# The next image's attention as side work inside a selective scan, with the depthwise taps on TensorE

## The chip, the cores and the metric

The kernel runs on one core of one Trainium2 chip. A time is the device time of one execution in microseconds. Three executions of the kernel before took 20170.54, 20181.5 and 20199.03 us; the time before is their median, 20181.5 us. One further execution was taken by the profiler, and all rows of the profile come from it.

## The reference

The input is a batch of 8 images of 384 channels and 64 x 64 positions, in fp32. Two layers follow each other, each added to its input.

Layer 0 is a channel attention on the group-normalised image (32 groups of 12 channels):

```python
q = dwconv3x3(conv1x1(gn(x), wq), dwq)      # likewise k and v; 9 taps per channel
q, k = l2norm(q), l2norm(k)                 # along the 4096 positions
attn = softmax(q @ k.T * temperature)       # 8 heads of 48 x 48 channels
x = x + conv1x1(attn @ v, wproj)
```

Layer 1 is a selective scan over the positions in four directions k (rows, columns, rows backward, columns backward):

```python
u = cross_scan(gn(x))                       # 4 directions x 384 channels x 4096 positions
dt, B, C = split(x_proj @ u)                # 12, 16, 16 rows
dt = softplus(dt_proj @ dt + dt_bias)
h = h * exp(dt * A) + (dt * u) * B          # for each of 16 states, position after position
y = sum over states of h * C, plus Ds * u
x = x + gelu(layernorm(cross_merge(y)))
```

## The kernel before

Channels lie on 128 partitions in three blocks (NJ = 3). The images are worked off one after the other: `channel_attention(b)`, then `selective_scan(b)`. The last step of an image (layer norm over channels, GELU, addition, store: `token_norm` and `finish_part`) is worked off inside the attention of the next image, through `emit`, and for the last image by `finish` at the end.

**Attention.** The whole image x lies in SBUF (three tiles of 4096 positions). `conv` multiplies x by the weights on TensorE (PE), into one of three PSUM banks `pc` (line 226), and ScalarE (ACT) copies with the bias into `pre` (line 231). The nine taps of the depthwise convolution are mainly multiply-adds on VectorE (DVE), one instruction for each tap and stretch of rows (line 266); for parts of the image the three taps of the middle column are matmuls with diagonal matrices on PE (line 249). `to_tokens` transposes (line 290), the gram matrix of q and k is summed on PE (line 327), and `project_out` multiplies, adds to x and takes statistics (lines 375 to 382). x1, the result, stays in SBUF and is stored for the finish.

**Scan.** An image has 32 steps: 4 directions times 8 chunks of 512 positions. A step has 12 units: 3 channel blocks times 4 groups of 4 states. A step's projection is `px` (line 474: for each of four stretches of 128 positions, matmuls with the x_proj weights of 44 columns; x is read in place, for odd k with a stride of 64), a copy to `xd`, `pd` (line 527: three matmuls of 128x512 with dt_proj) and softplus (line 535) to `dt`. GpSimd (POOL) computes `w` = dt * u (line 544). B comes back through DRAM as a copy on every partition (`fetch`, line 518), C as a spread tile `cp` (line 512). One unit u is:

- `drive`: POOL multiplies w by four rows of B, 128x2048 (`db`, line 573)
- `decay`: ACT computes four exponentials (`da`, line 561), in three PSUM banks
- `scan`: DVE runs four scans of 512 positions (`h`, line 585)
- `turn`: PE transposes h of the unit before, four sets of four transposes (`pt`, line 606), in two PSUM banks
- `keep`: ACT copies each set to SBUF (`hc`, line 614; one set of 48 in a step by DVE, line 616)
- `add_up`: PE multiplies each set by `cp` with 32 columns and sums in `py` (line 627; line 633 adds the term Ds * u with the matrix `skip`)

`take` adds py to what lies in DRAM (`ys`, `yd`, lines 655, 669, 653). `unit(u)` writes the order out by hand, and `tc.keep_in_program_order` holds every engine to it. Unit r = 9 of a step is the burst, in which the next step's pd and softplus run, with two table loads on ACT. A matmul in fp32 is two records in the profile, a transpose one.

Of the kernel before, what the change touches and what calls it, by code (L numbers as in the profile page):

```python
# [9 lines left out]
F32 = mybir.dt.float32  # L10
# [5 lines left out]
P = 128  # L16
C = 384
# [12 lines left out]
XR = R + 2 * N  # L30
# [49 lines left out]
def tile_channel_attention_then_selective_scan(ctx: ExitStack, tc: tile.TileContext, a: dict):  # L80
# [5 lines left out]
    big = ctx.enter_context(tc.tile_pool(name="big", bufs=1))  # L86
# [22 lines left out]
    for j in range(NJ):  # L109
        nc.vector.tensor_scalar_mul(skip[:, j, :], ident, d_sum[:, j : j + 1])  # L110

# [53 lines left out]
    def channel_attention(b, x, stats, before):  # L165
# [5 lines left out]
        with ExitStack() as st:  # L171
# [175 lines left out]
            emit = None  # L347
            if before is not None:
                scale, shift = token_norm(b, wp, work, before[2])

                def emit(i):
                    t = work.tile([P, L], F32, tag="acc", name=f"fin{b}_{i}")
                    room = [t[:, n * FT * NJ : (n + 1) * FT * NJ] for n in range(3)]
                    finish_part(*before, i, scale, shift, room, ps_t, "pt")

# [13 lines left out]
            x1_d = dram.tile([NJ, P, L], F32, tag="x1d", bufs=2, name=f"x1d{b}")  # L369
# [16 lines left out]
            todo, left, edges = [], list(range(L // FT)) if emit else [], {}  # L386
            for y0, y1 in zip(parts, parts[1:]):
                for m in range(NJ):
# [11 lines left out]
                    for _ in range(min(len(left), 2)):  # L400
                        emit(left.pop(0))
# [5 lines left out]
    def selective_scan(b, x1, stats1):  # L407

        y_d = dram.tile([L, C], F32, tag="yd", bufs=2, name=f"yd{b}")
        with ExitStack() as st:  # L410
            wp = st.enter_context(tc.tile_pool(name=f"sw{b}", bufs=1))
            work = st.enter_context(tc.tile_pool(name=f"s{b}", bufs=2))
            ps_y = st.enter_context(tc.tile_pool(name=f"sy{b}", bufs=2, space=PSUM))
            ps_a = st.enter_context(tc.tile_pool(name=f"sa{b}", bufs=3, space=PSUM))
            ps_t = st.enter_context(tc.tile_pool(name=f"st{b}", bufs=2, space=PSUM))
            ps_m = st.enter_context(tc.tile_pool(name=f"sm{b}", bufs=1, space=PSUM))
            pin = tc.keep_in_program_order

            wx = wp.tile([P, NJ, K, XR], F32, name=f"wx{b}")
            nc.sync.dma_start(wx, a["x_proj"])  # L420

            wdt = wp.tile([P, K, C], F32, name=f"wdt{b}")
            nc.gpsimd.memset(wdt, 0.0)  # L423
            nc.sync.dma_start(wdt[:R], a["dt_proj"])
            xd_bufs = [wp.tile([P, CH], F32, name=f"xd{b}_{i}") for i in range(2)]
            for t in xd_bufs:
                nc.gpsimd.memset(t, 0.0)

            with tc.tile_pool(name=f"sn{b}", bufs=1) as np_:
                mean, rstd = norm_factors(np_, ps_t, stats1, f"1_{b}", "t")  # L430
                shift = np_.tile([P, NJ], F32, name=f"shift{b}")
                nc.vector.tensor_mul(shift, mean, rstd)
                nc.vector.tensor_scalar_mul(shift, shift, -1.0)
                for c in range(NCH):
                    for j in range(NJ):
                        s = x1[j][:, bass.ts(c, CH)]
                        if c < 2:
                            nc.scalar.activation(  # L438
                                s, s, AF.Identity, bias=shift[:, j : j + 1],
                                scale=rstd[:, j : j + 1],  # L440
                            )
                        else:
                            nc.vector.tensor_scalar(
                                s, s, mean[:, j : j + 1], rstd[:, j : j + 1],
                                ALU.subtract, ALU.mult,
                            )

            def view(t, k, c):

                if k % 2 == 0:  # L450
                    return t[:, bass.ts(c, CH)].rearrange("p (x y) -> p x y", y=W)
                return t.rearrange("p (h w) -> p w h", w=W)[:, bass.ts(c, CH // H), :]

            def split(t):
                return t.rearrange("p (x y) -> p x y", y=W)

            steps = []
            for k in range(K):
                order = range(NCH) if k < 2 else range(NCH - 1, -1, -1)
                steps += [(k, c, i == 0, i == NCH - 1) for i, c in enumerate(order)]  # L460
            S = len(steps)
            UN = NJ * NG
            U = S * UN
            pxs, xds, bc_ds, cxs, pcts, cps, dts, ws, bts = {}, {}, {}, {}, {}, {}, {}, {}, {}

            def project(s, i):

                j, f = divmod(i, PX)
                k, c = steps[s][:2]
                if i == 0:  # L470
                    pxs[s] = ps_m.tile([P, CH], F32, tag="m", name=f"px{b}_{s}")
                n = CH // W // PX
                part = slice(f * n, (f + 1) * n)
                pin(nc.tensor.matmul(  # L474
                    split(pxs[s][:XR, :])[:, part, :], lhsT=wx[:, j, k, :],
                    rhs=view(x1[j], k, c)[:, part, :], start=i == 0, stop=i == PX * NJ - 1,
                ))

            def lay_out(s):

                xd = xd_bufs[s % 2]
                pin(nc.scalar.copy(xd[:XR, :], pxs.pop(s)[:XR, :]))  # L482
                bc_d = dram.tile([2 * N, CH], F32, tag="bcd", bufs=3, name=f"bcd{b}_{s}")
                nc.sync.dma_start(bc_d, xd[R:XR, :])
                cx = work.tile([NG * NQ, NV, HP], F32, tag="cx", bufs=1, name=f"cx{b}_{s}")
                for g in range(NG):
                    nc.sync.dma_start(
                        cx[g * NQ : (g + 1) * NQ],
                        bc_d[N + NV * g : N + NV * (g + 1), :].rearrange("v (q l) -> q v l", l=HP),
                    )  # L490
                xds[s], bc_ds[s], cxs[s] = xd, bc_d, cx

            def mingle_c(s):

                cy = work.tile([NG * NQ, HP, NV], F32, tag="cy", bufs=1, name=f"cy{b}_{s}")
# [3 lines left out]
            def turn_c(s):  # L499

                pcts[s] = ps_m.tile([P, CH], F32, tag="m", name=f"pct{b}_{s}")
# [5 lines left out]
            def spread_c(s, g):  # L507

                t = work.tile([P, NQ, HP], F32, tag="cp", bufs=5, name=f"cp{b}_{s}_{g}")
# [5 lines left out]
            def fetch(s, g):  # L515

                bts[s, g] = work.tile([P, NV, CH], F32, tag="B", bufs=NG, name=f"B{b}_{s}_{g}")
# [4 lines left out]
            def step_matmul(s, j):  # L522

                k = steps[s][0]
                pool, tag = (ps_m, "m") if j == 0 else (ps_t, "t")
                pd = pool.tile([P, CH], F32, tag=tag, name=f"pd{b}_{s}_{j}")
                pin(nc.tensor.matmul(  # L527
                    pd, lhsT=wdt[:, k, bass.ts(j, P)], rhs=xds[s], start=True, stop=True
                ))
                return pd  # L530

            def step_size(s, j, pd):
                k = steps[s][0]
                dts[s, j] = work.tile([P, CH], F32, tag="dt", bufs=4, name=f"dt{b}_{s}_{j}")
# [384 lines left out]
```

## Time and profile before

| what | us |
|---|---|
| median of three runs (20170.54 to 20199.03) | 20181.5 |
| the profiled execution's own time | 20193.86 |
| its span, first to last instruction | 20192.0 |
| first scan instruction (line 585) of image 0 and of image 1 | 488.2 and 2998.1 |
| scan of one image (488 to 2515) | 2027 |
| attention of one image with the finish of the image before (2515 to 2998) | 483 |
| after the last scan (20085 to 20192) | 107 |

In a row of a group, "busy" is the time in which at least one of its instructions ran, and "mean ns" the mean length of one. PE is the matmuls, PEld the loads of the weights that go before them. A row "A <- B" of the waits says that an instruction of A stood idle until one of B was done. A row of the timeline has the start, the length, the engine, the line, the operation with its tiles and how many instructions are merged in it; PE's rows can overlap, since a matmul's tail runs beside the next one.

### The profile page before, as it was taken

What the parts mean: (1) busy time and instruction counts of PE and PEld (TensorE: products, weight loads), DVE (VectorE), ACT (ScalarE), POOL (GpSimd) and SP (SyncE); (2) the same over time, 40 slices, a digit from 0 to 9 for tenths busy, and PEclk for the clock granted to TensorE, in tenths of its full rate; (3) what the DMA queues carried; (4) which work ended last, traced back from release to release, by engine and by line L of the source; (5) the groups of instructions that cost most, each with busy time, mean ns of one, the idle gap of its engine ahead of it and who ended that gap; (6) DMA issues with size and microseconds to landing.
All of it is one profiled execution on the core that took longest, in us unless ns stands there. A gap on an engine that the chain in (4) does not pass through costs nothing. (4 is left out here: it accounts for less than half of the span.)

```text
span 20192.0 us, 414595 instructions
## 1 busy us (share of the span) xinstructions
PE 17186.0 (85%) x167376; PEld 10318.0 (51%) x167376; DVE 18980.5 (94%) x17326; ACT 16767.4 (83%) x29099; POOL 15497.8 (77%) x6798
## 2 busy tenths in 40 slices
PE   7888888888888888888888888888888888888887
PEld 4555545555455544555545554455554555445554
DVE  7999989999899998999989999899998999989998
ACT  3999849998499985999859998599985999859998
POOL 0999909998099981999819998199971999729997
PEclk9999989999899999999999999899999999999998
DMA  1222322223222232222322223222232222322223
GB/s 43 84 95 94 99 78 84 94 95 101 75 84 95 94 105 78 84 94 96 103 74 85 95 94 102 74 85 95 94 102 74 85 95 95 102 75 85 94 94 121
DMA packets 1194159, 1814.03 MB, mean 90 GB/s; under 512 B 153552, under 2 KB 1018064, under 8 KB 1055024
## 3 DMA queue, kind: packets, MB, share of 16 engines
q1 hardware_dynamic: 1191376, 1787.38, 26.2%
q8 instruction: 1320, 21.63, 0.4%
q14 instruction: 599, 4.91, 0.1%
q10 hardware_dynamic: 864, 0.12, 0.0%
HBM read 1468.39 MB, written 318.77 MB: 89 GB/s over the span
## 5 line engine op out<-in xcount | busy, mean ns | idle before, releaser
L573 POOL TENSOR_TENSOR db<-w,B 128x2048 f32<-128x2048 f32 x3072 | 14052.0, 4575 | 722.1 <-DVE h L585 464.4
L585 DVE TENSOR_TENSOR_SCAN h<-da,ca,db 128x512 f32<-128x512 f32 x10752 | 12866.7, 1266 | 22.8 <-ACT da L561 18.6
L606 PE MATMUL pt<-ident,h 128*128 128x128 f32 x49152 | 7992.9, 291 | 1584.8 <-DVE h L585 1141.6
L561 ACT ACTIVATE da<-dt,neg_a 128x512 f32<-128x512 f32 x12288 | 8670.0, 706 | 635.3 <-DVE h L585 625.7
L614 ACT COPY hc<-pt 128x512 f32<-128x512 f32 x12040 | 7184.3, 597 | 661.6 <-PE pt L606 559.4
L606 PEld LDWEIGHTS pt<-ident,h 128*128 128x128 f32 x49152 | 5372.2, 144 | 4019.1 <-issue 2581.0
L627 PE MATMUL py<-hc,cp 128*32 128x128 f32 x98304 | 5045.2, 288 | 622.5 <-ACT hc L614 427.8
L627 PEld LDWEIGHTS py<-hc,cp 128*32 128x32 f32 x98304 | 2042.6, 109 | 2890.3 <-issue 1528.8
L423 POOL MEMSET wdt<- 128x1536 f32 x8 | 11.0, 1378 | 3559.6 <-DMA x1d<-x 3559.6
L585 DVE TENSOR_TENSOR_SCAN h<-da,db 128x512 f32<-128x512 f32 x1536 | 1749.6, 1206 | 14.7 <-ACT da L561 12.7
L474 PE MATMUL px<-x,wx 128*44 128x128 f32 x6144 | 1210.3, 341 | 28.9 <-ACT x L438 28.9
L544 POOL TENSOR_TENSOR w<-x,dt 128x512 f32<-128x512 f32 x744 | 1053.6, 1416 | 137.1 <-ACT dt L535 136.5
L474 PEld LDWEIGHTS px<-x,wx 128*44 128x44 f32 x6144 | 686.7, 128 | 356.4 <-issue 170.8
L512 DVE TENSOR_TENSOR cp<-quad,pct 128x512 f32<-128x512 f32 x1024 | 677.1, 663 | 45.3 <-PE pct L502 45.3
L527 PE MATMUL pd<-xd,wdt 128*128 128x512 f32 x1536 | 702.4, 593 | 5.8 <-ACT xd L482 5.8
L375 PE MATMUL pp<-v,mT 128*128 128x512 f32 x1152 | 548.0, 629 | 120.9 <-DVE v L266 57.3
L616 DVE COPY hc<-pt 128x512 f32<-128x512 f32 x248 | 171.6, 692 | 435.4 <-PE pt L606 435.4
L599 POOL COPY ca<-h 128x4 f32<-128x4 f32 x2688 | 520.5, 194 | 0.0
L535 ACT ACTIVATE dt<-pd,dt_bias 128x512 f32<-128x512 f32 x768 | 473.4, 685 | 5.0 <-PE pd L527 1.4
L375 PEld LDWEIGHTS pp<-v,mT 128*128 128x128 f32 x1152 | 226.4, 203 | 396.2 <-issue 306.0
L669 DVE TENSOR_TENSOR ys<-ys,py 128x512 f32<-128x512 f32 x576 | 388.6, 675 | 14.7 <-PE py L627 9.5
L527 PEld LDWEIGHTS pd<-xd,wdt 128*128 128x128 f32 x1536 | 271.4, 190 | 254.0 <-issue 128.9
(375 smaller groups left out, 11305.5 us busy)
## 6 DMA issues: line engine op xcount, KB each, us to landing
B<-bcd SPq DMA_DIRECT2D x1024, 1024.0 KB, 6.7
yd<-ys SPq DMA_DIRECT2D x384, 256.0 KB, 2.3
ys<-yd SPq DMA_DIRECT2D x768, 128.0 KB, 3.0
yd<-ys SPq DMA_DIRECT2D x768, 128.0 KB, 2.5
x<-in_x SPq DMA_DIRECT2D x48, 1024.0 KB, 7.2
x1d<-x SPq DMA_DIRECT2D x192, 256.0 KB, 2.0
ys<-yd SPq DMA_DIRECT2D x192, 256.0 KB, 2.9
fy<-yd SPq DMA_DIRECT2D x128, 384.0 KB, 3.8
```

Source lines behind the costliest of these rows:

```text
L375: nc.tensor.matmul(pc, lhsT=mT[:, j, bass.ts(m, P)], rhs=v[:, j, bass.ts(c, CH)], start=j == 0, stop=j == NJ - 1,)
L474: pin(nc.tensor.matmul(split(pxs[s][:XR, :])[:, part, :], lhsT=wx[:, j, k, :], rhs=view(x1[j], k, c)[:, part, :], start=i == 0, stop=i == ...
L512: pin(nc.vector.tensor_mul(t, m.broadcast_to([P, NQ, HP]), c.broadcast_to([P, NQ, HP])))
L527: pin(nc.tensor.matmul(pd, lhsT=wdt[:, k, bass.ts(j, P)], rhs=xds[s], start=True, stop=True))
L544: pin(eng.tensor_mul(split(ws[s, j]), view(x1[j], k, c), split(dts[s, j])))
L561: pin(nc.scalar.activation(t, dts[s, j], AF.Exp, scale=neg_a[:, j, steps[s][0], n : n + 1]))
L573: pin(eng.tensor_mul(t, w.broadcast_to([P, NV, CH]), bts[s, g]))
L585: pin(nc.vector.tensor_tensor_scan(h, da, db, 0.0 if start else carries[s - 1][:, j, n : n + 1], ALU.mult, ALU.add,))
L599: pin(nc.gpsimd.tensor_copy(carries[s][:, j, NV * g : NV * (g + 1)], hs[u][:, e, :]))
L606: pin(nc.tensor.transpose(t[:, f, :], hs[u][:, bass.ts(q, HP), :].rearrange("p l v -> p (l v)"), ident))
L614: pin(eng.copy(t, src))
L627: pin(nc.tensor.matmul(py[f * HP : (f + 1) * HP, lb, :], lhsT=cps[s, g][:, q, :], rhs=hc[:, f, :], start=g == lb == 0, stop=g == NG - 1 an ...
```

## The change

Image 0's attention is as before, without the finish of an image before. Then `first_image` normalises x1 and writes two planes to DRAM, `xr` in row order and `xc` in column order (POOL copies the turned image). One `stream` scans all 256 steps of the 8 images. A step's u is brought from a plane (`bring`, one step ahead of its projection) and is contiguous for every direction. During the scan of image b the attention of image b + 1 runs as a list of small pieces, `attention(b + 1)`, each with a cost; four times in a unit `rest(slot)` calls `ending` (the finish of image b - 1, one chunk of 512 positions in a step, in steps 1 to 8) and `aside`, which issues pieces until the share of costs reaches the share of slots (1480 slots for an image, the last 14 units have none). A piece marked `fresh` starts a slot of its own.

In the side work all nine taps are matmuls with diagonal matrices, which `build_taps` makes on POOL at the start and stores to DRAM; 9 are accumulated for each block of 128 channels and 512 positions. x, v, the transposed k and x1 go through DRAM. All matmuls of the side work share one PSUM bank (`bank()`), taken from the exponentials, which now have two. The square roots of the side work are an Ln and an Exp on ACT and a step of refinement on DVE. The projection's weights have 128 columns, with dt's rows at partitions 0, 32 and 64, so that the three pd matmuls read 32 rows each; the keep that DVE did goes to ACT, and the GELU of a finish stands in the burst.

```diff
+    def build_taps():
+        with tc.tile_pool(name="taps", bufs=2) as pool:
+            for w, n in enumerate("kqv"):
...
+                    for i in range(9):
+                        nc.gpsimd.tensor_scalar_mul(t[:, i, :], ident, dw[:, m, i : i + 1])
+                    nc.sync.dma_start(taps_d[w, m], t)
...
+    def root(r, v):
+        pin(nc.scalar.activation(r, v, AF.Ln))
+        pin(nc.scalar.activation(r, r, AF.Exp, scale=-0.5))
...
+    def first_image(x, stats1):
...
+                    nc.sync.dma_start(rows_d[j, :, bass.ts(c, CH)], s)
...
+                    nc.gpsimd.tensor_copy(t, turn_image(x[j])[:, bass.ts(i, W * TP // L), :])
+                    nc.sync.dma_start(cols_d[j, :, bass.ts(i, TP)], t.rearrange("p w h -> p (w h)"))
...
-            ps_a = st.enter_context(tc.tile_pool(name=f"sa{b}", bufs=3, space=PSUM))
+            ps_a = st.enter_context(tc.tile_pool(name="sa", bufs=2, space=PSUM))
+            ps_g = st.enter_context(tc.tile_pool(name="sg", bufs=1, space=PSUM))
...
+            def bring(s):
...
+                us[s] = work.tile([P, NJ, CH], F32, tag="u", bufs=2, name=f"u_{s}")
+                nc.sync.dma_start(
+                    us[s], planes[b][k % 2][:, :, bass.ts(c, CH)].rearrange("j p l -> p j l")
+                )
...
-                    split(pxs[s][:XR, :])[:, part, :], lhsT=wx[:, j, k, :],
-                    rhs=view(x1[j], k, c)[:, part, :], start=i == 0, stop=i == PX * NJ - 1,
+                    pxs[s][:, part], lhsT=wx[:, j, k, :], rhs=us[s][:, j, part],
+                    start=i == 0, stop=i == PX * NJ - 1,
...
-                    pd, lhsT=wdt[:, k, bass.ts(j, P)], rhs=xds[s], start=True, stop=True
+                r = slice(HP * j, HP * (j + 1))
+                pin(nc.tensor.matmul(pd, lhsT=wdt[r, k, :], rhs=xds[s][r, :], start=True, stop=True))
...
+                def load_band(i):
+                    s_["xb"] = new("xb", [P, NJ, CH])
+                    nc.sync.dma_start(s_["xb"], x_d[b, :, :, bass.ts(i, CH)].rearrange("j p l -> p j l"))
+
+                def conv_keep(m, i):
...
+                    pin(nc.scalar.activation(
+                        s_["pre"][:, bass.ts(i, CH)], s_["g"], AF.Identity, bias=s_["bias"][:, m : m + 1]
+                    ))
...
+                def tap_mm(i, n):
...
+                    mm(g3[:, r0 - y0 : r1 - y0, x0:x1], s_["dg"][:, tap, :],
+                       p3[:, r0 + dy : r1 + dy, x0 + dx : x1 + dx], n == 0, n == 8)
...
+                for which in "kqv":
+                    weights(which)
+                    do(0, load_band, 0)
+                    for m in range(NJ):
+                        do(0, load_taps, which, m)
...
+                        for i in range(NCH + 1):
+                            if i < NCH:
+                                for j in range(NJ):
+                                    do(0.86, conv_mm, m, j)
+                                do(0.1, conv_keep, m, i, fresh=True)
+                                if i < NCH - 1 or m < NJ - 1:
+                                    do(0, load_band, (i + 1) % NCH)
+                            if i > 0:
...
+                                for n in range(9):
+                                    do(0.86, tap_mm, i - 1, n)
+                                do(0.1, tap_keep, fresh=True)
...
+                                do(0.5, turn_acc, fresh=True)
+                                do(0.1, keep_turned, fresh=True)
+                                do(0.1, square, i - 1, fresh=True)
...
+                                    for t in range(4):
+                                        do(0.33, gram_mm, m, t)
+                                    do(0.1, gram_add, m, i - 1, fresh=True)
...
+            SLOTS = (SI - 2) * UN * NV + 10 * NV
+
+            def aside(u, slot):
...
+                goal = side["total"] * side["t"] / SLOTS
+                first = True
+                while side["todo"] and (side["done"] < goal or side["t"] >= SLOTS):
+                    cost, fresh, fn, args = side["todo"][-1]
+                    if fresh and not first and side["t"] < SLOTS:
+                        break
+                    side["todo"].pop()
+                    side["done"] += cost
+                    fn(*args)
+                    first = False
...
                 kept(0)
                 turned(1)
+                rest(0)
...
                 kept(1)
...
                 turned(2)
                 added(0)
+                rest(1)
                 scanned(2)
                 decay(i0 + 4)
                 kept(2)
                 turned(3)
                 added(1)
...
+                rest(2)
                 scanned(3)
                 decay(i0 + 5)
                 kept(3)
                 added(2)
+                rest(3)
...
-    for b in range(B):
-        x1, x1_d, stats1 = channel_attention(b, *x, before)
-        y_d, x = selective_scan(b, x1, stats1)
-        before = (b, x1_d, y_d)
-    finish(*before)
+    build_taps()
...
+        x1, x1_d, stats1 = channel_attention(0, *x)
+        planes0 = first_image(x1, stats1)
+    x1_d, y_d = stream(planes0, x1_d)
+    finish(x_d.shape[0] - 1, x1_d, y_d)
```

## The prediction

> **What bounds the kernel now.** I read the page's busy row first, then stages by windows, then the waits, then PE's timeline, because the change moves work onto PE. The page's row names no idle engine:
>
> ```profile
> PE 17186.0 (85%) x167376; PEld 10318.0 (51%) x167376; DVE 18980.5 (94%) x17326; ACT 16767.4 (83%) x29099; POOL 15497.8 (77%) x6798
> ```
>
> Cut into the first image's scan and the second image's attention (columns: span, busy us of PE, PEld, DVE, ACT, POOL, then PE's clock):
>
> ```profile
> 488.00:2515.00 2027.00, 1748.10 (x19585) 1065.87 (x19585) 1966.74 (x1804) 1873.26 (x3224) 1926.27 (x843) 0.97 0.27 92
> 2515.00:2998.00 483.00, 395.98 (x1337) 221.14 (x1337) 405.25 (x363) 222.88 (x413) 10.97 (x7) 0.88 0.25 84
> ```
>
> The scan is bound by DVE (97%), with POOL (95%) close behind. Attention takes 483 us an image, 316 of them the depthwise taps on DVE (line 266 in that window), and POOL idles. One image is 2510 us (first scans begin at 488.2 and 2998.1). The waits from 600 to 2400 us (total us, times, longest) agree: DVE waits for nothing, PE waits for DVE.
>
> ```profile
> DVE h L585 <- ACT da L561: 3.2, 12, 0.4
> ...
> PE pt L606 <- DVE h L585: 123.6, 148, 1.4
> ...
> PE pt L606 <- ACT dt L535: 31.2, 28, 1.2
> ```
>
> So the question is how much of PE is free in the scan. Busy time counts the tails of pipelined matmuls; starts do not (start us, length, then records):
>
> ```profile
> 498.80 1.09 PE L606 MATMUL pt<-ident,h 128*128 128x128 f32 x8
> 499.82 0.43 PE L627 MATMUL py<-hc,cp 128*32 128x128 f32 x8
> 500.18 0.49 PE L633 MATMUL py<-skip,x 128*128 128x128 f32 x2
> 500.50 0.60 PE L606 MATMUL pt<-ident,h 128*128 128x128 f32 x4
> ...
> 503.11 0.66 PE L606 MATMUL pt<-ident,h 128*128 128x128 f32 x4
> 503.69 0.85 PE L474 MATMUL px<-x,wx 128*44 128x128 f32 x6
> 504.48 0.66 PE L606 MATMUL pt<-ident,h 128*128 128x128 f32 x4
> 505.06 0.43 PE L627 MATMUL py<-hc,cp 128*32 128x128 f32 x8
> 505.42 0.66 PE L606 MATMUL pt<-ident,h 128*128 128x128 f32 x4
> 506.00 0.64 PE L627 MATMUL py<-hc,cp 128*32 128x128 f32 x16
> 506.58 0.66 PE L606 MATMUL pt<-ident,h 128*128 128x128 f32 x4
> ...
> 1007.99 1.48 PE L474 MATMUL px<-x,wx 128*44 128x128 f32 x6
> 1009.39 0.66 PE L606 MATMUL pt<-ident,h 128*128 128x128 f32 x4
> ...
> 2364.70 2.74 PE L527 MATMUL pd<-xd,wdt 128*128 128x512 f32 x6
> 2367.37 0.64 PE L627 MATMUL py<-hc,cp 128*32 128x128 f32 x16
> ...
> 2681.74 19.05 PE L226 MATMUL pc1q<-x,wq 128*128 128x512 f32 x44
> ```
>
> From start to start: a turn of four transposes 0.58 before another shape, two turns in a row 1.02, a sum of 8 records 0.36, of 16 0.58. A unit has four turns and four sums: 0.58 + 0.36 + 1.02 + 0.36 + 0.58 + 0.58 = 3.48 us. A step has 12 (41.8), four px groups that split a pair of turns (0.58 + 0.79 + 0.58 - 1.02 = 0.93 each, 3.7; where k is odd px takes 1.40, so 6.2), pd 2.7, skips 1.2, pct 0.2: 49.6 us, or 52.1 for odd k. Times 16 and 16: 1627 us of PE per image's scan. The last row is PE's full rate: 19.05/44 = 0.433 us a record, two records or 0.866 us for a 128x512 matmul.
>
> **The change, part by part, on PE.**
>
> Scan. u is now contiguous, so odd px becomes as short as even: 49.6 x 32 = 1587. The most it could give: px at the dense rate (24 x 0.108 = 2.6 instead of 3.7) and the three pd, now on 32 rows each, side by side in 1.0 instead of 2.7, as the four 32-column matmuls of a sum evidently are (8 records in 0.36): 1497. For a loss I see no reason beyond the old 1627. I take 1560, nearest to the even row.
>
> Side work per image: conv 216 x 0.866 = 187; taps 648, a third of 512 columns and the rest of 504 or a border row less, 549; projection out 72, 62; 192 transposes at 0.109 (8 in 0.87 between starts), 21; gram 64 of 144 columns and 32 of 192 (16 records in 1.96 and 2.60), 26; 96 transposes of the finish, 10; biases, means and fold, 18. Sum 873 us.
>
> Shape changes. The third of the four slots of a unit lies between two sums that go as one x16 today: 0.36 + 0.36 - 0.58 plus about 0.17 into the side matmul is 0.3 us, in two of three units (965 of the 1480 slots of an image hold a matmul): 70 us (0 to 110).
>
> Together 1560 + 873 + 70 = 2503 us of PE per image, against 2510 that an image takes now. PE becomes the bound, and full before it waits at all.
>
> The side list does not load PE evenly. The statistics of x and the writing of the two planes fill about 80 of 1480 slots (20 units) with no matmul, and the last 14 units of an image have no slot: there a unit stays at DVE's 5.28 us while PE needs 4.06. 34 x 1.2 = 41 us. That makes 2544.
>
> Waits that PE, in order, adds, with scan transposes queued behind each:
> - load_band has one buffer. Band 1 is loaded in the same slot that multiplies it, 9 times an image, and band 0 at the head of k, q and v: 12 loads of 768 KB on SP's queue. Neighbours: 576 KB 3.7 us, 1024 KB 7.2 us. 12 x 5 = 60 (0 to 90). The other loads are issued nine taps ahead, some 13 slots or 23 us; SP's queue, which they join, stands up to 19 us today before a store of ys (828 us in those 1800), so they just hide; half of 72 late by 3 would be 110, and I take nothing.
> - One PSUM bank serves all side work. In 72 places the first tap follows the ACT copy of the same slot (0.69 us, of which a turn hides half), in some 48 a DVE add: 50 (0 to 150). PE's waiting keeps ACT's next keeps late too.
> - The burst: 31.2 us of waiting for dt in 1800 today is 1.1 a step. The keep that DVE did goes to ACT, behind softplus and, in 8 steps of 32, Gelu and its 1.28 us table load: 50 (0 to 120).
> - 16 roots an image, two table loads each, 41 us on ACT, and scale_w behind POOL's 4.57 us multiplies: nothing, since ACT and POOL have slack below; without that cover 90.
>
> Sum 160 (0 to 560). An image takes 2704 us.
>
> The Trainium skill ("Perfetto Trace Analysis", Matmuls) asks that independent matmul groups rotate through PSUM banks so that copying one out overlaps the next; it gives no price. The old conv with three banks ran 44 records without a hole; no row here shows a single bank, so the 50 us above is not from the page.
>
> Others, off that path: DVE 1967 - 17 (its keep) + 24 x 0.69 of statistics, 24 x 1.4 in projection, some 40 of small ones = 2040. ACT 1873 + 240 copies at 0.6 and tables = 2100. POOL 1926 + 12 turns of the image at 2.6 (512 elements take 1.29) + 32 scalings and 8 adds, some 95, = 2020. All below 2544, hence no bound.
>
> Head: tap tiles are built and stored before x may load into the same memory: 81 POOL operations between 0.2 (a 128x128 memset) and 0.4, then nine stores: 50 us (25 to 90). The planes of image 0: 12 POOL turns and their stores ahead of the first u: 42 (25 to 60). The first scan then starts at 580. After the last scan starts, today's 20192 - 18057 = 2135 us stay, plus 20 for the finish of image 6 beside it.
>
> 580 + 7 x 2704 + 2155 = 21663 us of span. The profiled execution's own time is 20193.9, 2 above its span and 12 above the median, so about 21650 by the median. At 2494 an image the change breaks even.
>
> **A rule that says otherwise.** PE's row shows 1748 busy of 2027 but PEld 1066. The Trainium skill ("Trainium Kernel Development and Optimization", Performance Expectations) calls matmul busy time a bad measure of what is left and points to weight loads. By that PE would be half free and all 873 us would hide behind DVE's 2040: an estimate of 580 + 7 x 2040 + 2155 = 17015. It is right that busy overstates, by 121 us. But in the dense row a load takes 0.19 of each 0.433 us: the array is full at 44%, so I go by starts.
>
> **The rivals.**
> - PE has more room than starts show (faster). Each change between 128*128 and 128*32 leaves 0.17 to 0.20 us without a load, 8 in a unit; if side matmuls fill them, 8 x 0.18 x 384 = 550 us come free. For: no wait stands there. Against: the skip at 500.18, a 128*128 shape behind a sum, starts 0.36 after it like any turn, so the gap moves. It decides from 210 us an image on (0.07 a gap, with every wait as summed); at half, 2430 an image and 19745 us.
> - PE full, waits hidden (no change): 2490 an image, 20165 us. The 160 would have to vanish, against 31.2 and 123.6 seen today with a less loaded PE.
> - The in-order waits dominate: PE, ACT and DVE each wait for the other within a slot, 460 of the 560: 3004 an image, 23763 us. Against: a unit of h in advance covers stalls of some 3 us on DVE.
> - That side work is not spread but flushed at an image's end: the last slot holds one item, so I give it nothing.
>
> **How the numbers follow.** PE bound with some waits: 0.74, of which time 21650. Waits dominate: 0.10. No change: 0.05. More room: 0.11. Within 0.2% is what a measurement can tell here (runs spread 20171 to 20199). The range leaves out the faster case below and some 0.09 above: 20150 (2490 an image) to 22750 (2861). Faster 0.11, same 0.05, slower 0.84.
>
> **What would show it.** After: PE's busy share above 95% in a middle image, DVE near 75%; waits of DVE for da and of POOL for h long, of PE for h few; an image period of 2600 to 2850 against 2510; the last image back at DVE's pace; tap rows of two records at 0.43 each. Wrong if DVE stays above 90% in the middle images, if pt and py follow each other faster than 0.36 and 0.58, or if PE idles by over 400 us an image.

## The result and the profile after

Four executions of the changed kernel took 23714.83 to 23733.43 us, median 23731.19; four of the kernel before 20170.54 to 20199.03, median 20178.74. The ratio is 1.1757 [1.1737, 1.1777]: 17.6% slower. The forecast was 21650 (20150 to 22750). The direction held; the forecast is 2080 us too low, and the time lies above its range. The profiled execution took 23714.83 us, its span is 23713.0. Experiments below have one profiled execution each and are set against 23714.8; the four executions lie 19 us apart, and the kernel before, run once beside each group of experiments, took 20169.9 to 20198.9, so differences below some 30 us say nothing.

The page's busy row of the kernel after:

```profile
PE 20856.6 (88%) x175608; PEld 11806.1 (50%) x175608; DVE 17292.5 (73%) x16498; ACT 17361.6 (73%) x29612; POOL 16246.0 (69%) x7317
```

PE went up to 88% and is now the highest, DVE fell from 94 to 73%. The windows of image 0, of image 1 and of the last image's scans (span, busy us of PE, PEld, DVE, ACT, POOL, then PE's clock):

```profile
594.00:3462.00 2868.00, 2616.37 (x21930) 1468.11 (x21930) 2072.31 (x1945) 2103.95 (x3611) 1959.09 (x870) 0.95 0.36 118
3462.00:6447.00 2985.00, 2665.56 (x22116) 1495.72 (x22115) 2132.30 (x2054) 2172.70 (x3708) 2036.31 (x912) 0.93 0.36 120
21382.00:23613.00 2231.00, 1849.06 (x19745) 1142.80 (x19745) 2008.76 (x1865) 1997.87 (x3350) 1991.07 (x884) 0.89 0.29 100
```

An image is 2985 us instead of the forecast 2704 (and of 2510 before); image 0, which has no image before it to finish, 2868. The miss of 2050 us in the span is 14 us of head (the first scan starts at 594.5), 164 in image 0, 6 x 283 in images 1 to 6, and 176 from the last image's first scan on (23713 - 21382 = 2331 against 2155).

The waits of image 1, from 3462 to 6447 (total us, times, longest), PE first, then the longest of DVE, ACT and POOL:

```profile
PE py L656 <- ACT hc L645: 97.3, 86, 5.4
PE pt L637 <- ACT hc L645: 85.3, 59, 6.8
PE g L812 <- ACT pre L911: 35.3, 26, 7.1
PE g L812 <- DMA xb<-in_x: 34.0, 9, 5.4
PE pt L637 <- ACT dt L567: 25.8, 24, 2.1
...
DVE h L616 <- ACT da L592: 566.1, 426, 9.1
...
ACT hc L645 <- PE pt L637: 474.3, 419, 9.1
ACT da L592 <- DVE h L616: 249.3, 200, 6.6
...
POOL db L604 <- DVE h L616: 698.2, 271, 14.0
```

Before, DVE hardly waited and PE waited mostly for DVE. Now everyone waits along the ring PE, ACT, DVE, POOL. All of PE's rows add up to 314 us, 188 of them for `hc`, ACT's copy of the transposed states. The rest of the image, 2985 - 314 = 2671 us, PE is at work. That is 168 more than the 2503 of the forecast.

PE's timeline in a full unit says that the forecast's cadences (the times from start to start) were right (start us, length, then records):

```profile
4007.59 0.60 PE L637 MATMUL pt<-ident,h 128*128 128x128 f32 x4
4008.12 0.42 PE L656 MATMUL py<-hc,cp 128*32 128x128 f32 x8
4008.47 0.66 PE L637 MATMUL pt<-ident,h 128*128 128x128 f32 x4
4008.97 1.01 PE L812 MATMUL g<-pre,dg 128*128 128x504 f32 x2
4009.81 0.83 PE L507 MATMUL px<-u,wx 128*128 128x128 f32 x6
4010.48 0.60 PE L637 MATMUL pt<-ident,h 128*128 128x128 f32 x4
...
4013.71 1.11 PE L812 MATMUL g<-pre,dg 128*128 128x504 f32 x2
4014.66 0.60 PE L637 MATMUL pt<-ident,h 128*128 128x128 f32 x4
```

From 4007.59 to 4014.66 are 7.07 us with three side matmuls, one px group and no wait. By the forecast's terms it is 3.48 for the unit, 0.30 for the shape change and 3 x 0.866, and px takes 0.67 here (the forecast had 0.93 where px splits a pair of turns): 7.05. So at full speed the instructions are not dearer. Where the 168 us come from shows in a burst that holds a Gelu, ACT and PE from 3649 on:

```profile
3649.83 1.28 ACT L567 ACT_TABLE_LOAD   x1
...
3651.12 1.85 ACT L567 ACTIVATE dt<-pd,dt_bias 128x512 f32<-128x512 f32 x3
...
3652.44 1.24 PE L637 MATMUL pt<-ident,h 128*128 128x128 f32 x8 [0.16 <-ACT dt L567]
...
3652.99 1.28 ACT L749 ACT_TABLE_LOAD   x1
...
3654.28 2.22 ACT L749 ACTIVATE fz<-fz,ln_b,ln_w 128x512 f32<-128x512 f32 x3
...
3656.52 1.28 ACT L592 ACT_TABLE_LOAD   x1
...
3658.45 0.58 ACT L645 COPY hc<-pt 128x512 f32<-128x512 f32 x1
...
3659.07 0.65 PE L656 MATMUL py<-hc,cp 128*32 128x128 f32 x8 [5.40 <-ACT hc L645]
...
3659.66 3.78 PE L812 MATMUL g<-xb,wt 128*128 128x512 f32 x4
...
3663.23 0.92 PE L637 MATMUL pt<-ident,h 128*128 128x128 f32 x4
3664.08 0.43 PE L656 MATMUL py<-hc,cp 128*32 128x128 f32 x8
```

For 8 us ACT does nothing that the units of the running step wait for. PE stands 5.40 us behind one copy, and the work after it is slow: four records of 128x512 from 3659.66 to 3663.23, 0.89 us each where a record takes 0.433; the set of transposes behind them still 0.85 to the next start instead of 0.53; then the pace is back. The windows of this stretch have the granted clock in the third column from the end:

```profile
3656.00:3662.00 6.00, 2.92 (x11) 1.38 (x12) 2.73 (x3) 5.78 (x10) 1.89 (x2) 0.59 0.64 250
3662.00:3668.00 6.00, 6.00 (x43) 3.25 (x45) 3.06 (x3) 3.70 (x7) 1.23 (x1) 0.84 0.13 24
```

Cut into slices of 5 us, with (1 - granted clock) weighted by PE's busy time in each slice, image 1 loses 146 us at half speed, an estimate from the clock column; the old scan of 2027 us lost 41, where DVE set the pace.

The Trainium skill ("TensorE: Matmul & The Clock Gate", Part 1, What's actually happening) says that TensorE falls to half its clock after an idle window of some 3.4 us and comes back after a window of work. The burst agrees with that. The section's figure of under 1% of a typical span is for the first ramp; here the waits and the half speed come back all the time, and 146 of 2985 us are 5%.

### The profile page after: what moved, and what is told of

Its sections match the earlier page's. It is cut to its first block, busy times and chain, and to the rows that moved or that the text cites. A ratio compares the mean times of both kernels' runs of the same rounds, so it can differ in the third digit from the quotient of the medians.

```text
span 23713.0 us, 432883 instructions
## 1 busy us (share of the span) xinstructions
PE 20856.6 (88%) x175608; PEld 11806.1 (50%) x175608; DVE 17292.5 (73%) x16498; ACT 17361.6 (73%) x29612; POOL 16246.0 (69%) x7317
## 5 line engine op out<-in xcount | busy, mean ns | idle before, releaser
L637 PEld LDWEIGHTS pt<-ident,h 128*128 128x128 f32 x49152 | 5862.5, 147 | 4489.4 <-issue 2742.3
L812 PE MATMUL g<-pre,dg 128*128 128x504 f32 (+3 forms) x10080 | 5573.2, 636 | 257.4 <-ACT pre L911 228.6
L812 PEld LDWEIGHTS g<-pre,dg 128*128 128x128 f32 x10080 | 1542.0, 193 | 1009.3 <-issue 632.1
L812 PE MATMUL g<-xb,wt 128*128 128x512 f32 x3024 | 1765.6, 690 | 292.2 <-DMA xb<-in_x 238.5
L575 POOL TENSOR_TENSOR w<-u,dt 128x512 f32<-128x512 f32 x765 | 978.6, 1279 | 764.2 <-ACT dt L567 764.2
L507 PEld LDWEIGHTS px<-u,wx 128*128 128x128 f32 x6144 | 841.1, 198 | 297.0 <-issue 297.0
L507 PE MATMUL px<-u,wx 128*128 128x128 f32 x6144 | 882.6, 282 | 46.9 <-DMA u<-xr 46.9
L812 PEld LDWEIGHTS g<-xb,wt 128*128 128x128 f32 x3024 | 543.5, 211 | 720.8 <-issue 603.3
L729 POOL TENSOR_SCALAR fy<-fy,fmv,frs 128x384 f32<-128x384 f32 x224 | 366.5, 1652 | 386.2 <-issue 272.1
L561 PE MATMUL pd<-xd,wdt 32*128 32x512 f32 x1536 | 462.4, 657 | 37.3 <-ACT hc L645 34.8
```

The source lines that it names most:

```text
L507: pin(nc.tensor.matmul(pxs[s][:, part], lhsT=wx[:, j, k, :], rhs=us[s][:, j, part], start=i == 0, stop=i == PX * NJ - 1,))
L561: pin(nc.tensor.matmul(pd, lhsT=wdt[r, k, :], rhs=xds[s][r, :], start=True, stop=True))
L575: pin(eng.tensor_mul(ws[s, j], us[s][:, j, :], dts[s, j]))
L637: pin(nc.tensor.transpose(t[:, f, :], hs[u][:, bass.ts(q, HP), :].rearrange("p l v -> p (l v)"), ident))
L812: pin(nc.tensor.matmul(out, lhsT=lhsT, rhs=rhs, start=start, stop=stop))
```

## The experiments

**Leaving parts out.** Four kernels leave out the finish of images 0 to 6, the attention of images 1 to 7, both, or eight of nine tap matmuls.

```diff
 e1_no_finish, e3_bare
-                        ending(s, r, slot)
...
-                        fin_gelu(b - 1, i - 1)
 e2_no_side, e3_bare: attention(b) for b > 0
+                planes[b], x1_ds[b] = planes0, x1_d0
+                return todo
 e4_one_tap
                     tap = order[n]
+                    if n > 0:
+                        return
...
```

> Leaves out the finish of images 0 to 6 inside the stream (their layer norm, GELU, addition and store; image 7 is finished as before). In the changed kernel image 0, which has no finish beside it, takes 2868 us, the six after it 2987, the last 2231 up to its last scan. Theory F (the finish, 10 us of PE, costs what ACT's table loads and POOL's scalings hold up): all seven at 2868, the last near 2140, in all 594 + 7 x 2868 + 2140 + 100 = 22900 us. Rival P (PE's amount of work sets the time, the finish hides as I had priced it, some 34 us an image): 23490 us.

> Leaves out the whole attention of images 1 to 7 (every scan reads the planes of image 0); the stream, its two banks for the exponentials and the finish stay. Theory P (PE's amount sets the time): PE has room again, DVE sets the pace at 2028 as before, 594 + 8 x 2035 + 107 = 16980 us. Theory W (the order in which ACT, PE and DVE wait for each other costs time even when none of them is full): images with a finish go on at the 2231 of the last image, 594 + 2140 + 7 x 2231 + 100 = 18450 us.

> Leaves out both, the attention of images 1 to 7 and the finish of images 0 to 6: the bare stream of scans. If the stream alone is as fast as the scan stage before (2027 an image), 594 + 8 x 2027 + 107 = 16920 us. If it is slower by itself (two banks for the exponentials instead of three, the ninth unit's keep on ACT), as the last 1500 us of the last image suggest (DVE 92% busy there against 97% before), 2140 an image and 17820 us.

> Leaves out eight of the nine tap matmuls (576 of 936 large matmuls of an image), with costs, slots, copies, loads and all waits as they are. Theory P (PE full): an image loses 576 x 0.866 to 0.94 = 500 to 541 us and takes about 2460, 23730 - 7 x 520 = 20090 us. Theory W (waits): PE's removed work was partly cover for waiting on ACT; less than two thirds return, 21400 us or more. If DVE's pace with side work were the only limit left, 2240 an image, 18600 us.

Measured: 22945.2, 18430.0, 17599.3 and 21542.8 us. The finish costs 770 us or 110 an image, though it has only some 10 us of PE by the forecast (its transposes are busy for 15). The attention costs 5285 or 755 an image; before, the whole stage with the finish in it took 483. The bare stream takes (17597.5 - 594.5 - 107)/8 = 2112 us an image against 2027 of the old scan. The eight taps give back 310 us an image of the 490 or so that they occupy PE: the rest went into waiting and half speed, as the table below shows, and the clock is only 0.895 then. The second and the fourth speak against PE's amount of work as the only term; they do not yet tell what the rest is.

**The exponentials' PSUM bank.** The change gives the side work a bank that the exponentials had. e5 gives it back in the bare stream; e9 gives it back in the whole change and takes one from `py`; e12 issues each exponential one slot earlier besides; e18 takes the bank from the kernel before.

```diff
 e5_bare_da3, e9, e12
-            ps_a = ... tc.tile_pool(name="sa", bufs=2, space=PSUM)
+            ps_a = ... tc.tile_pool(name="sa", bufs=3, space=PSUM)
 e9_y1_da3, e12: the take of the burst moves ahead of added(0), and
-            ps_y = ... tc.tile_pool(name="sy", bufs=2, space=PSUM)
+            ps_y = ... tc.tile_pool(name="sy", bufs=1, space=PSUM)
 e12_y1_da3_lead3, in all slots
-                decay(i0 + 2)
+                decay(i0 + 3)
 e18_before_da2
-            ps_a = ... tc.tile_pool(name=f"sa{b}", bufs=3, space=PSUM)
+            ps_a = ... tc.tile_pool(name=f"sa{b}", bufs=2, space=PSUM)
```

> Finish of images 0 to 6 and attention of images 1 to 7 left out, as in the bare stream, and the exponentials of the scan get three PSUM banks again instead of two (the side work's bank is free). Theory B (the missing bank is what makes the bare stream 2112 us an image instead of the old scan's 2027: ACT's next exponential waits for a DVE scan to free a bank): back to some 2030 an image, 16950. Rival (the burst, in which ACT does one copy more and DVE waits up to 3.8 us, or the u loads, make it): 17400 to 17600.

> The whole change, but with three PSUM banks for the exponentials, bought with one bank less for the sums of y (PE then waits for DVE to take the last sum, three times a step; in the burst the take is moved ahead of the sum). Theory B (two banks lock ACT's exponentials to DVE's scans, and with side work all stalls pass through this lock): 85 us an image or more come back, 23050 or less; the 242 us in 2900 that ACT waits for DVE's h are gone. Rival (ACT's exponentials are late because they stand behind copies that wait for PE, so a bank more changes nothing): 23500 to 23900.

> The whole change with three PSUM banks for the exponentials (one for the sums of y), and each exponential issued one slot earlier: three scans ahead instead of two, so that a copy on ACT that waits for PE no longer stands right before the exponential that DVE needs next. Theory W (DVE's wait for da comes from ACT's order: hc waits for PE's transposes, da stands behind hc): DVE waits far less and 60 us an image or more come back beyond the bank alone (23201): 22750 or less. Theory P (PE's own work and its half-speed stretches set the period, the waits only show who is early): 23100 to 23250, with DVE waiting elsewhere.

> The kernel before, with two PSUM banks for the exponentials instead of three, nothing else. If the lost bank is a price of its own in the scan, as in the bare stream (56 us an image): 20550 to 20680 against some 20180. If it only costs in the new order: 20170 to 20250.

Measured: 17151.6 (448 less than e3, 56 an image), 23200.7 (514 less, 64 an image), 23654.7 (60 less) and 20547.3 against 20198.9 beside it (348 more, 44 an image). e5 and e9 fell between their two ranges, e12 above both. So the bank has a price with or without side work (the 64 are net of what the bank taken from `py` costs) and accounts for two thirds of the bare stream's 85; the other 29 stay unexplained. In the waits of 3600 to 6400, DVE's first row and ACT's two, after, e9 and e12 in this order:

```profile
DVE h L616 <- ACT da L592: 544.2, 415, 9.1
ACT hc L645 <- PE pt L637: 459.0, 406, 9.1
ACT da L592 <- DVE h L616: 216.3, 167, 6.6
```

```profile
DVE h L616 <- ACT da L592: 486.8, 367, 7.9
ACT hc L645 <- PE pt L637: 535.4, 489, 9.8
ACT da L592 <- DVE h L616: 70.4, 92, 4.6
```

```profile
DVE h L616 <- ACT da L592: 279.2, 211, 7.9
ACT hc L645 <- PE pt L637: 460.1, 411, 9.2
ACT da L592 <- DVE h L616: 215.6, 165, 6.8
```

e12 is the telling one: DVE's largest wait was halved (part of it stands now in other rows) and the time is nearly that of the kernel after. What e9 won and e12 gave back is ACT's wait for DVE: with as many banks as exponentials in advance, ACT stands until a scan has freed one, and the copies that PE waits for stand behind it. PE's own waits in image 1 go with the time: 188 us for `hc` after, 131 in e9 (which waits 27 more for `h`), 185 in e12. The theory that DVE's wait for late exponentials sets the period falls.

**Who stands behind whom.** e8 moves the 216 side copies an image from ACT to DVE, e7 four of nine taps back to DVE.

```diff
 e8_keeps_dve (likewise conv_keep and keep_turned)
-                    pin(nc.scalar.copy(s_["acc"], s_["g"]))
+                    pin(nc.vector.tensor_copy(s_["acc"], s_["g"]))
 e7_dve_taps4: after tap_keep, for the last four taps
+                    pin(nc.vector.scalar_tensor_tensor(
+                        o, p3[:, r0 + dy : r1 + dy, x0 + dx : x1 + dx],
+                        dw_all[which][:, m, tap : tap + 1], o, ALU.mult, ALU.add,
+                    ))
```

> The side work's PSUM copies of conv, taps and turned taps (216 an image, 0.6 to 0.7 us each) go from ACT to DVE. Theory A (ACT's queue is what delays the exponentials: each side copy stands ahead of one): 140 us an image less on ACT, of which the scan gets 60 to 110 back: 22950 to 23300. Rival (the copies only wait for PE wherever they stand; on DVE they hold up scans instead): 23700 to 24300.

> Four of the nine taps go back to DVE (multiply-adds on the kept sum, 288 an image, some 0.55 us each like the old taps on DVE); PE has 288 x 0.84 = 242 us an image less, DVE 158 more (2290 of the present 2987). Theory P (PE's amount of work sets the period): 242 less an image, 22040. Theory W (the order of the queues sets most of it: leaving eight taps out returned 60%): 145 less at most, 22700 and above; if the multiply-adds in DVE's queue hold up scans, no gain: 23500 to 24300.

Measured: 23791.0 (76 more) and 25351.6 (1637 more, above both its ranges). Taking the copies off ACT gains nothing where DVE has to make them instead. e7 says nothing on PE's share, because its price was wrong: the multiply-adds took 1.42 us in the mean, not 0.55, 410 us of DVE an image. DVE and POOL from 4995 on show why:

```profile
4995.21 0.71 DVE L942 SCALAR_TENSOR_TENSOR acc<-pre,dwa_q,acc 128x504 f32<-128x504 f32 x1
...
4997.27 4.87 POOL L608 TENSOR_TENSOR db<-w,B 128x2048 f32<-128x2048 f32 x1 [3.13 <-DVE h L620]
4997.68 1.27 DVE L620 TENSOR_TENSOR_SCAN h<-da,ca,db 128x512 f32<-128x512 f32 x1
4998.88 3.80 DVE L942 SCALAR_TENSOR_TENSOR acc<-pre,dwa_q,acc 128x504 f32<-128x504 f32 x1
5002.09 0.64 POOL L634 COPY ca<-h 128x4 f32<-128x4 f32 x1
```

The same tap takes 0.71 us or, begun beside POOL's multiply, until half a microsecond after that has ended (5002.68 against 5002.14). A scan is not held up (1.27). The old taps ran while POOL was idle.

**PE's own terms.** e6 moves the third slot's side work ahead of the sum, so that the two sums run as one again; e15 leaves out 63 of the 72 loads of a band an image.

```diff
 e6_slot2
                 turned(3)
+                rest(2)
                 added(1)
...
-                rest(2)
                 scanned(3)
 e15_xb_once
+                    if i > 0:
+                        return
                     s_["xb"] = new("xb", [P, NJ, CH])
```

> The third slot's side work goes ahead of the sum of the unit instead of between two sums, so the two sums run as one again. Theory P (PE is full, every shape change counts; I priced these at 0.3 us in two of three units, 70 us an image): 23150 to 23300. Theory W (PE has 10% to spare, what counts is who stands behind whom; the sum stands behind one matmul more): 23650 to 23850.

> Of the 72 loads of a band of x for conv 63 an image are left out (the first band is used for all), so that PE does not wait for one. PE waited 34 us an image for them, 9 times. Theory K (a wait costs itself and half speed after it): 45 to 60 us an image, 23300 to 23400. Rival (it costs what it waits, or less since others catch up): 23450 to 23700.

Measured: 23271.9 (443 less, 63 an image, where the forecast had 70 for the shape changes) and 23414.0 (301 less, 43 an image, for 34 us of waiting). This saving of PE's work comes back nearly whole, so PE, with what it waits for, sets the period; and the wait that is taken away gives back 1.26 times its length. e15 lies between its two ranges, 14 us from the first; the table below shows the two parts of its gain.

**The finish.** e10 leaves out its Gelu, roots and polishing, e11 POOL's scaling and the last addition.

```diff
 e10_fin_noact (also without the polish)
-                        fin_gelu(b - 1, i - 1)
...
-                        root(fin["rs"], fin["tm"])
+                        pin(nc.vector.tensor_copy(fin["rs"], fin["tm"]))
 e11_fin_nopool
-                        fin_scale(b, i, slot)
...
-                pin(nc.gpsimd.tensor_add(fin["z"], fin["z"], fin["x"]))
```

> Of the finish of images 0 to 6 the Gelu and the two roots' Ln and Exp on ACT (with their table loads) and the polishing on DVE are left out; loads, statistics, scaling on POOL, transposes, copies and the final add stay. Leaving out the whole finish gave 786 us, 112 an image. Theory T (ACT's table loads in the burst stall the scan: 8 steps an image, each with a Gelu table, three Gelus and two root tables, some 7 us of ACT): 50 to 80 an image, 23180 to 23380. Theory O (POOL's scaling, 4 x 1.65 us beside its multiplies, and the final add of 128x1536): 23500 to 23700.

> Of the finish of images 0 to 6 POOL's part is left out: the four scalings by mean and root, 1.65 us each, and the add of x1 before the store; the rest stays. Theory O (POOL's multiplies db come late behind these, and DVE's scans with them): 50 to 80 us an image less, 23180 to 23380. Theory T (it is ACT's table loads): 23600 to 23750.

Measured: 23286.5 (428 less, 61 an image) and 23758.2 (43 more). More than half of the finish's 110 comes from ACT's part (with DVE's polishing), which is 52 us of work an image (in all seven 124 of Gelu, 216 of 168 table loads at 1.28, 23 of Ln and Exp); taking away POOL's 1.65 us scalings gains nothing. The remaining 49 us are not separated.

**Half speed, and whether the terms add.** e14 puts idle multiplications into every burst, right before the sum that waits for ACT; e17 only into those with a Gelu; e13 joins e9 and e6, e16 e14 as well.

```diff
 e14_warm (e17_warm_gelu: 6 or none)
                     kept(3)
+                    idle = ps_m.tile([P, CH], F32, tag="m", name=f"idle_{u}")
+                    for n in range(6 if b > 0 and 0 < i <= NCH else 2):
+                        pin(nc.tensor.matmul(idle, lhsT=ident, rhs=us[s][:, 2, :], start=True, stop=True))
                     added(2)
```

> The whole change, and in the burst of each step PE gets idle multiplications (128x512, result unused) right before the sum that waits for ACT's copy behind softplus and Gelu: 6 where a Gelu is in the burst (there it waits 5.4 us), 2 elsewhere; 83 us of PE work more an image. Theory K (PE pays for a wait twice: after 5.4 us of waiting four records took 3.78 instead of 1.73 us, half speed for some 4 us; the granted clock of 0.93 is worth 170 us an image): more work makes it faster, 20 to 60 us an image, 23250 to 23570, clock above 0.94. Rival (half speed is only seen where nobody needs PE, or it depends on more than the wait before): the added work costs or changes nothing, 23700 to 24300.

> The whole change with the 6 idle multiplications only in the 56 bursts that hold a Gelu, where PE waits 5.4 us anyway (5.2 us of work put into the wait, 42 us an image). Theory K (half speed after the wait costs some 2 us each time): 100 to 150 us less in all, 23560 to 23615. Rival (half speed after a wait costs nothing in the end): 23690 to 23760.

> Two of the edits together: three banks for the exponentials with one for the sums of y (it gave 513 us by itself) and the third slot's side work ahead of the sum (441 by itself). If PE's time is a sum of work and waits, as theory P with half-speed stretches says, they add: 22700 to 22850. If they take up the same slack: 23000 to 23200.

> All three: three banks for the exponentials, the third slot's work ahead of the sum, and idle multiplications in the burst. If all add: 22250 to 22700. It stays above the kernel before by either theory: at 2494 us an image it would be even, and this is some 2800.

Measured: 23636.7 (78 less, clock 0.949 instead of 0.929), 23659.1 (56 less, 0.936), 22833.8 (881 less; e9 and e6 add to 957) and 22779.4 (another 54). PE in e14 at the burst that was shown above:

```profile
3659.94 1.24 PE L637 MATMUL pt<-ident,h 128*128 128x128 f32 x8 [0.16 <-ACT dt L567]
3661.01 5.32 PE L1301 MATMUL idle<-u,ident 128*128 128x512 f32 x12
3666.58 0.43 PE L656 MATMUL py<-hc,cp 128*32 128x128 f32 x8 [0.25 <-ACT hc L645]
3667.06 1.12 PE L812 MATMUL g<-xb,wt 128*128 128x512 f32 x2
```

The copy came just as late, but the two records behind it are done in 1.12, at full pace. 83 us of useless work an image made the kernel a little faster: half speed after a wait is a cost. The times of e14 and e17 miss both expected ranges all the same, and e16 lies 79 us above its own: e17 gives 1.0 us back for each of its 56 bursts where some 2 were expected. Image 1 of each run, from its first scan to that of image 2, shows where the rest went (PE's waits are the sum of its rows; the last column is the account from the clock, as above):

| run | image 1, us | PE waits | PE occupied | of it lost at half speed |
|---|---|---|---|---|
| after | 2985 | 314 | 2671 | 146 |
| e9 | 2918 | 281 | 2637 | 122 |
| e12 | 2980 | 312 | 2668 | 143 |
| e15 | 2939 | 288 | 2651 | 127 |
| e4 | 2674 | 406 | 2268 | 208 |
| e14, 83 of it idle work | 2973 | 261 | 2712 | 102 |
| e17, 42 of it idle work | 2974 | 282 | 2692 | 121 |

In e17 the loss at half speed falls by 25 us, 3 a burst, but the 42 us of idle work replace only 32 of waiting, so that the image gains no more than 11. In e14 the loss falls by 44, and 83 us of idle work replace 53. In e15 the waits fall by 26 and the loss by 19. In e4 the waits grow by 92 and the loss by 62, which is most of what its taps did not give back. The 146 us as a whole stay an account, as no run took all of it away.

## Why the prediction was right in direction and wrong in size

The steps that failed are two terms of the sum for an image: the waits that PE adds, put at 160 us, and PE's work, priced at full speed throughout. In their place the runs show 314 us of waits (against 201 with the uneven slots) and some 146 us lost at half speed after such waits.

- **PE becomes the bound: right, with its waits.** e6 shows it for a small saving; of e4's larger one 310 us of 490 came back. Of the signs, PE's busy share in a middle image is 89%, not above 95; DVE has 71%; DVE's waits for `da` and POOL's for `h` are long and PE's for `h` few (6.6 us), and tap rows and the cadences are as written; the period of 2985 lies outside 2600 to 2850, and the last image is not back at DVE's pace (2231 us, DVE busy 90% of it).
- **Work of 2503 at full clock: right in its terms.** The full unit takes 7.07 against 7.05, the shape changes 63 against 70. Missing was the clock: the rows came from a scan at 0.97, and I priced all work at that speed. PE was occupied for 2671; 146 of the 168 us are accounted for by half speed, the other 22 stay open.
- **Waits of 160, with 41 for uneven slots 201: mis-sized, 314.** The side work's single bank was right (rows of `g` behind ACT and DVE add up to 49, against 50), the band loads were 34 against 60. Wrong was the burst at 50 and the sentence that the roots and their tables cost "nothing, since ACT and POOL have slack below". Waits for `hc` and `dt` are 214. ACT's slack is a mean over the image (2173 of 2985); in the burst it is in order, and PE stands behind it. Sorted by their times, some 86 of the 214 lie in the 32 bursts and 50 beside the 16 roots; the other 78 lie elsewhere, and no run separates their cause. The price "without that cover 90" was there and should have been taken: e10 gives 61 for ACT's part of the finish alone.
- **Two waits of the kernel before were passed over.** The views of 600 to 2400 that the forecast quotes also have these rows, so DVE did wait, and PE already stood behind ACT's copies:

```profile
DVE hc L616 <- PE pt L606: 49.8, 29, 2.5
...
PE py L627 <- ACT hc L614: 48.3, 75, 0.8
```

- **The bank was not priced at all.** That the exponentials go from three banks to two stood in the diff. It costs 64 us an image (e9), 44 in the old kernel (e18). This is no third term beside waits and half speed but lies within them: in image 1 of e9 PE waits 33 us less and is occupied 34 less, 24 of these by the clock. The last image has no side attention and shows it too: its scans take 2226 us, 2172 with the bank back (e9) and 2097 without the finish beside it (e1), which the forecast had put at 20. A slip of 10 us stands in that term besides: before, the last image's scans begin at 18067.4, not at 18057.
- **The rule on weight loads** gave 17015 and is off by 6700: PEld is at 50% in a kernel that PE bounds.
- **The rival "in-order waits dominate"** named 23763 and the time is 23731, but not by its mechanism: it needed 460 us of waits beside the 41, PE has 314 in all, and halving DVE's waits moved nothing. The 314 us of waits and the 168 that PE is occupied longer come to 482, so that its number lies near is luck.

No version beats the kernel before: the best of them, e16, takes 22779 us, and 2494 us an image would be needed.

## What to carry to other kernels

Sum PE's cadences at full clock only for stretches without waits; every wait of some microseconds on an in-order queue ahead of PE was paid here once as waiting and again in part at half speed, so find the longest single occupation (here 8 us of tables and Gelu on ACT) and not the mean slack. A large wait on the page need not be the one to remove: take one away, and see whether the engine that sets the period gets its work sooner. Count buffers that a change takes from the old work like instructions that it adds.

## What the chip showed that was not expected

- TensorE ran four records of 128x512 in 3.78 us right after a wait of 5.40 us, against 1.73 at the dense rate; the granted clock over 3656 to 3662 was 0.59. With idle work in the wait this was gone.
- A multiply-add of DVE on two SBUF operands took 0.71 us alone and up to 3.80 beside POOL's multiply of 4.87. The Trainium skill ("SBUF — State Buffer", SBUF: two separate sides) describes such an exclusive lock between DVE and GpSimd; this run agrees.
- What counts for the exponentials is how many banks there are beyond the scans in advance: 2 banks and 2 in advance took 23714.8, 3 and 3 nearly the same 23654.7, but 3 banks and 2 in advance 23200.7 (the last two with one bank less for `py`).
